# Four graph layers in one program: sources renamed to node ranks, table rows written by plain transfers, the MLP's bias added on VectorE, and the background work put in another order

## The chip, the cores and the metric

The kernel runs on one core of one Trainium2 chip. The metric is the device time of one execution in microseconds (us). Before the change three runs gave a median of 8303.18 us, the lowest 8277.47 and the highest 8350.5.

## The reference, cut to what matters

There are 6250 nodes with 128 features and 100000 edges, sorted by target. Four layers follow each other. Each takes `h = relu(layernorm(x))` and adds its result to `x`.

```python
# layer 0: graph attention, 8 heads, softmax over the edges of one target
x = layernorm(h) * gamma + beta;  x = x @ W_in + b_in
e = leaky_relu((x @ W_u + b_u)[src] + (x @ W_v)[dst])
probs = softmax of e over the edges with the same dst
out = segment_sum(x.reshape(N, 16, 8)[src] * probs[:, None, :], dst).reshape(N, 128) @ W_ff + b_ff
# layer 1: graph convolution with self loops, then batch norm over the nodes and relu
out = segment_sum((x @ W)[src] * dinv[src] * dinv[dst], dst) + b
out = relu((out - mean) * rsqrt(var + eps) * gamma + beta)
# layer 2: twice a one-head attention with self loops (W1, as1, ad1, b1), relu, (W2, as2, ad2, b2)
out = segment_sum(h[src] * softmax_by_dst(leaky_relu(alpha_s[src] + alpha_d[dst])), dst) + bias
# layer 3: a message is weighted by an edge MLP, and is summed at the SOURCE of the edge
w = silu(attr32 @ rad_W1 + rad_b1) @ rad_W2 + rad_b2 + silu(attr4 @ sph_W1 + sph_b1) @ sph_W2 + sph_b2
alpha = (q[src] * w * k[dst]).sum over 32 / sqrt(32) * edge_weight * edge_weight_n2     # 4 heads
out = segment_sum(alpha * v[dst], src)
```

## The kernel before, in words

**Ranks and columns.** The function `survey` sorts the nodes by degree. A node's place in that order is its rank. The ranks are cut into NR = 49 blocks of 128 (the index b in every loop). `node_i[:, b]` holds the node numbers of block b. Block b is given CAPS[b] edge columns (44 for the first block, 25 for the second, 9 for the last), so a block's edges fill a rectangle of 128 ranks by CAPS[b]. There are TC = 820 columns in all. `places` fills `ell`, which holds for each column the node number of the source of each of the 128 edges, or a dummy. (If the edges don't fit, another path runs. It isn't taken here.)

**Stages.** `fast0_nodes` writes the table of layer 0 (and `xv`, the node features) in the order of nodes. After it come five loops over the 49 blocks:

- g0, L1363 to L1394: layer 0. `fetch` issues one indirect gather a column (L1037) from the table into `g_x`, of which there are two buffers. VectorE makes the softmax and the sum (L1370 to L1383). Two small products follow (`times`, with `normed` between them). `by_node` (L1027) scatters the 128 new rows into table t1 with an indirect transfer from GpSimd, since the rows' places go by `node_i`.
- g1, L1407 to L1416: layer 1's gather and sum (L1411), and the mean over the nodes. After it the batch norm (L1420 to L1444), which ends in a product and a scatter into t2 for each block.
- g2 and g3, L1447 to L1475: the two attentions of layer 2. g2 scatters into t3. g3 calls `pair_rows` (L1483), which reads the MLP's result for the block's edges (`pr_e`, L1503), multiplies it by k, and writes rows of 257 numbers [w*k, lane of the source, v] into `pair_rows` in HBM: one part from SP's queue (L1509), one from ScalarE's (L1510). It also scatters q and x into `after`.
- fp, `fast_pairs` L1513: 49 blocks of nodes. 18 gathers (L1522) fetch the pairs of a block by the list `ids`, a one-hot matrix `fp_oh` (L1526) is made, transposed on TensorE (L1534), multiplied by q (L1539), and the messages are summed by matmuls (L1547).

**Background.** Three generators are advanced from within the loops by `take(generator, n)`, n steps a block:

- `weights` (`edge_weights`, 400 steps) is the edge MLP. A step does two edges for each of 125 partitions: four matmuls into `ew_h` (L1211, L1212), two SiLUs on ScalarE (L1214), six matmuls into `ew_ay` (L1218, L1219, and L1220, which adds the bias as a product of a row of ones and the bias row), and two evictions on ScalarE that scale by the edge weights (L1221). `ew_ay` and `ew_h` have one PSUM buffer each. Every second step a transpose into `ew_ay` comes first (L1201).
- `spots` (`source_places`, some 100 steps) finds each edge's place in an order by source, on VectorE.
- `ids` (`source_rows`, 820 steps) turns those places into the gather list of fp: three VectorE operations (L1289, L1292, L1293) and four matmuls (L1296) a step, with two buffers for `sr_t` and `sr_l`.

Instructions of each engine run in the order that the framework's scheduler gives them when the program is built, so `take` only proposes a place. Each DMA queue (SP, ScalarE, GpSimd) is in order too.

Of the kernel before, what the change touches and what calls it, by code (L numbers as in the profile page):

```python
# [15 lines left out]
F32 = mybir.dt.float32  # L16
# [20 lines left out]
NH, HD = 8, 16  # L37
# [805 lines left out]
def survey(k, dst):  # L843


    nc, tc = k.nc, k.tc
# [3 lines left out]
    k.odd = k.keep.tile([1, 1], I32, name="odd")  # L850
    with tc.tile_pool(name="sv", bufs=1) as p:
# [98 lines left out]
        nc.vector.tensor_copy(rl, ri)  # L950
        with tc.tile_pool(name="sv4", bufs=1) as q, tc.tile_pool(name="sv4_ps", bufs=1, space=PSUM) as ps:
# [29 lines left out]
def places(k, src):  # L981

    nc, tc = k.nc, k.tc
    line = k.dram.tile([E + RUN, 1], I32, name="src_line")
    k.ell = k.fast.tile([128, TC], I32, name="ell")
    with tc.tile_pool(name="pl", bufs=1) as p:
# [46 lines left out]
def fetch(k, p, table, b, width, name, more=0):  # L1033

    x = p.tile([128, WM + more, width], F32, name=name, bufs=2)
    for j in range(CAPS[b]):
        k.nc.gpsimd.indirect_dma_start(  # L1037
            out=x[:, j, :], out_offset=None, in_=table,
            in_offset=bass.IndirectOffsetOnAxis(ap=k.ell[:, COL[b] + j:COL[b] + j + 1], axis=0))
    return x  # L1040
# [110 lines left out]
def edge_weights(k, c, ps, src, attr32, attr4, ew1, ew2, rw1, rb1, rw2, rb2, sw1, sb1, sw2, sb2):  # L1151
# [3 lines left out]
    k.edges = k.dram.tile([E + RUN, D + 1], F32, name="edge_rows")  # L1155
    z = c.tile([RUN, D + 1], F32, name="ew_z")
# [13 lines left out]
    b2, c2 = load_row(k, c, rb2, "ew_b2", 1), load_row(k, c, sb2, "ew_c2", 1)  # L1170
    nc.vector.tensor_tensor(b2, b2, c2, op=ALU.add)
    scale = c.tile([EP, EC], F32, name="ew_scale")
    lane = c.tile([EP, EC], F32, name="ew_lane")
    with tc.tile_pool(name="ew0", bufs=1) as q:
        w = q.tile([EP, EC], F32, name="ew_w")
        nc.sync.dma_start(scale, ew1.rearrange("(p c) -> p c", p=EP))
        nc.sync.dma_start(w, ew2.rearrange("(p c) -> p c", p=EP))
        nc.vector.scalar_tensor_tensor(scale, scale, float(D3) ** -0.5, w, op0=ALU.mult, op1=ALU.mult)
        i = q.tile([EP, EC], I32, name="ew_i")
        nc.scalar.dma_start(i, src.rearrange("(p c) -> p c", p=EP))  # L1180
        j = q.tile([EP, EC], I32, name="ew_j")
        nc.vector.tensor_scalar(j, i, 127, None, op0=ALU.bitwise_and)
        nc.vector.tensor_copy(lane, j)
# [4 lines left out]
    for c0 in range(0, EC, KC):  # L1188
# [5 lines left out]
        for t in range(0, KC, 2):  # L1194
# [9 lines left out]
            if t % KO == 0:  # L1204
                out = c.tile([EP, KO, D + 1], F32, name="ew_out", bufs=2)
                nc.vector.tensor_copy(out[:, :, D], lane[:, c0 + t:c0 + t + KO])
# [8 lines left out]
            for n in range(2):  # L1215
# [3 lines left out]
                nc.tensor.matmul(y, lhsT=g[:, 1, e], rhs=s2, start=False, stop=False)  # L1219
                nc.tensor.matmul(y, lhsT=k.ones[0:1, :EP], rhs=b2, start=False, stop=True)  # L1220
                nc.scalar.activation(out[:, t % KO + n, 0:D], y, AF.Identity, scale=scale[:, c0 + t + n:c0 + t + n + 1])  # L1221
            if (t + 2) % KO == 0:
                at = (c0 + t + 2 - KO) * (D + 1)
                by_engines(nc.sync.dma_start, to[:, at:at + KO * (D + 1)], out.rearrange("p c f -> p (c f)"))
            yield


def source_places(k, c, q, acc):
# [4 lines left out]
    k.lane3 = c.tile([128, TC], F32, name="sp_lane")  # L1233
    b = q.tile([128, TC], I32, name="sp_b")
    nc.vector.tensor_scalar(b, k.ell, 7, None, op0=ALU.logical_shift_right)
# [32 lines left out]
    w, x = q.tile([128, TC], I32, name="sp_w"), q.tile([128, TC], I32, name="sp_x")  # L1268
    nc.vector.tensor_copy(w, pos)
    nc.vector.tensor_scalar(x, w, 7, None, op0=ALU.logical_shift_right)  # L1270
    nc.vector.tensor_copy(k.tile3, x)
    nc.vector.tensor_scalar(x, w, 127, None, op0=ALU.bitwise_and)
    nc.vector.tensor_copy(k.lane3, x)
# [3 lines left out]
def source_rows(k, c, acc):  # L1277
# [9 lines left out]
    for cc in range(TC):  # L1287
        t = c.tile([128, TT], F16, name="sr_t", bufs=2)
        nc.vector.tensor_scalar(t, it, k.tile3[:, cc:cc + 1], None, op0=ALU.is_equal)  # L1289
        l = c.tile([128, 2, 128], F16, name="sr_l", bufs=2)  # L1290
# [21 lines left out]
def fast_layers(k, x, src, edges, l0, l1, l2a, l2b, l3, after):  # L1312
# [3 lines left out]
    with ExitStack() as ctx:  # L1316
# [9 lines left out]
        xp = c.tile([128, NR, D + NH], F32, name="xp")  # L1326
        own = c.tile([128, NR, D + 2], F32, name="own")
# [11 lines left out]
        for n, a in enumerate(l3[8:11]):  # L1339
            for h in range(H3):  # L1340
                s = slice(h * D3, (h + 1) * D3)
                nc.sync.dma_start(w4[s, n, s], a[h])
        k.pairs = k.dram.tile([(TC + 1) * 128, 2 * D + 1], F32, name="pair_rows")
        none = c.tile([128, 2 * D + 1], F32, name="pair_none")
        nc.gpsimd.memset(none, 0.0)
        nc.gpsimd.memset(none[:, D:D + 1], -1.0)
# [9 lines left out]
                               mlp.enter_context(tc.tile_pool(name="mlp_ps", bufs=1, space=PSUM)), src, *edges, *l3[0:8])  # L1356
# [3 lines left out]
        with tc.tile_pool(name="g0s", bufs=1) as ps0, \  # L1360
                tc.tile_pool(name="g0", bufs=2) as p, tc.tile_pool(name="g0_ps", bufs=2, space=PSUM) as ps:
            spots = source_places(k, later, ps0, places3)
            for b in range(NR):  # L1363
# [4 lines left out]
                rows = fetch(k, p, t0, b, D + NH, "g0_x")  # L1368
# [23 lines left out]
                by_node(k, t1, own[:, b, 0:D], b, "t1")  # L1392
                take(spots, 3)
                take(weights, 3)  # L1394
            take(spots, 3 * NR)

        ids = source_rows(k, later, places3)

        with tc.tile_pool(name="g1", bufs=2) as p:
# [5 lines left out]
            with tc.tile_pool(name="g1_st", bufs=1, space=PSUM) as ps1:  # L1405
                mean = ps1.tile([128, D], F32, name="g1_mean")
                for b in range(NR):  # L1407
                    n = CAPS[b]
                    rows = fetch(k, p, t1, b, D, "g1_x")
# [227 lines left out]
```

## Time and profile before

| What | Value |
|---|---|
| median of 3 runs | 8303.18 us |
| profiled execution: its own time, its span | 8362.09 us, 8360.3 us |
| PE, weight loads, DVE, ACT, POOL busy | 50%, 34%, 40%, 20%, 56% |
| mean granted TensorE clock | 0.627 |
| HBM | 420.83 MB read, 186.20 MB written, 73 GB/s |
| gathers by L1037 | 3280, mean 1.0 to 1.1 us on POOL |
| gathers by L1522 | 882, mean 1061 ns |

POOL is GpSimd, PE is TensorE, DVE is VectorE, ACT is ScalarE, SP is the sync engine whose queue issues plain transfers. Idle time of an engine is put down to what ended it. "issue" means that the profile shows nothing that the engine waited for. No engine is busy through the whole span, and the stages differ, so the table alone says little: times are to be read by stage.

### The profile page before, as it was taken

To read this page: it belongs to the slowest core of one execution; us is meant where nothing else is said; L and a number is where in the kernel's file an instruction comes from. 1 tells how busy PE (TensorE), PEld (TensorE's weight loads), DVE (VectorE), ACT (ScalarE), POOL (GpSimd) and SP (SyncE) were. 2 spreads that over 40 slices of the span, in tenths; PEclk is the share of its full clock that TensorE was granted. 3 is DMA by queue.
4 is the path that set the end of the run, shared out by engine and by line. 5 is a ranking of instruction groups with operands and counts; after the bars stand their busy time and mean duration, and the time that the engine had idled before them with its cause. 6 is when DMAs were issued, how large, how long until landed. Compare 5 with 4: busy or idle time off the path is not lost. (4 is left out here: it accounts for less than half of the span.)

```text
span 8360.3 us, 55810 instructions
## 1 busy us (share of the span) xinstructions
PE 4209.2 (50%) x17979; PEld 2860.6 (34%) x17979; DVE 3377.0 (40%) x6506; ACT 1638.4 (20%) x3582; POOL 4708.7 (56%) x4551
## 2 busy tenths in 40 slices
PE   2314555666466456766556789942100002554555
PEld 2213344443233334544333455620000002444444
DVE  9535455443222222434333454334433343434344
ACT  0202233332111111342222233301111111000000
POOL 0166777664545555345666761046777775667665
PEclk9555555667655555775555669965555555777777
DMA  0222222222111111122222221048888884333333
GB/s 4 67 47 51 56 58 56 54 55 41 50 43 50 44 48 50 42 47 50 48 55 51 59 52 39 27 70 162 163 156 164 153 162 104 93 92 93 93 93 81
DMA packets 440385, 611.13 MB, mean 73 GB/s; under 512 B 88306, under 2 KB 332388, under 8 KB 436487
## 3 DMA queue, kind: packets, MB, share of 16 engines
q0 software_dynamic: 164688, 409.60, 20.9%
q1 hardware_dynamic: 169128, 143.04, 8.1%
q10 hardware_dynamic: 106254, 54.71, 4.0%
q8 instruction: 147, 2.41, 0.1%
q14 instruction: 168, 1.37, 0.1%
HBM read 420.83 MB, written 186.20 MB: 73 GB/s over the span
## 5 line engine op out<-in xcount | busy, mean ns | idle before, releaser
L1037 POOL DMA_INDIRECT g_x<-l_t,ell x1640 | 1661.6, 1013 | 1066.4 <-issue 485.7
L1296 PE MATMUL sr_acc<-sr_t,sr_l 128*128 128x441 f16 x3280 | 1111.2, 455 | 567.2 <-DVE sr_l L1292 287.0
L1037 POOL DMA_INDIRECT g_x<-l2b_t,ell x820 | 898.0, 1095 | 765.7 <-DVE sr_l L1293 373.7
L1289 DVE TENSOR_SCALAR sr_t<-sr_it,sp_tile 128x882 f16<-128x882 f16 x820 | 378.1, 461 | 2204.9 <-PE sr_acc L1296 1032.4
L1522 POOL DMA_INDIRECT fp_rows<-pair_rows,ids x882 | 935.5, 1061 | 447.7 <-issue 260.6
L1037 POOL DMA_INDIRECT g_x<-l2a_t,ell x820 | 835.5, 1019 | 352.1 <-issue 262.6
L1218 PE MATMUL ew_ay<-ew_r,ew_g 128*125 128x128 f32 x1600 | 478.9, 394 | 954.9 <-issue 460.7
L1218 PEld LDWEIGHTS ew_ay<-ew_r,ew_g 128*125 128x125 f32 x1600 | 366.1, 266 | 1158.9 <-issue 520.4
L1221 ACT ACTIVATE ew_out<-ew_ay,ew_scale 125x128 f32<-125x128 f32 x800 | 293.8, 367 | 2237.0 <-remote 987.5
L1296 PEld LDWEIGHTS <-sr_l 128*128 128x128 f16 x3280 | 337.8, 117 | 928.6 <-DVE sr_l L1292 333.2
L1211 PE MATMUL ew_h<-ew_aT,ew_r 128*128 128x125 f32 x1600 | 516.9, 416 | 100.8 <-ACT ew_aT L1203 50.6
L1212 PE MATMUL ew_h<-ew_dT,ew_s 40*128 40x125 f32 x1600 | 522.0, 418 | 18.4 <-issue 11.0
L1220 PE MATMUL ew_ay<-ew_b,ones 1*125 1x128 f32 x1600 | 522.3, 418 | 0.0
L1061 PE MATMUL tm_ty<-ident,pr_h 128*128 128x128 f32 x49 | 22.4, 459 | 859.4 <-ACT pr_h L1054 545.0
L1219 PE MATMUL ew_ay<-ew_s,ew_g 128*125 128x128 f32 x1600 | 425.6, 360 | 5.3 <-ACT ew_g L1214 4.3
L1211 PEld LDWEIGHTS ew_h<-ew_aT,ew_r 128*128 128x128 f32 x1600 | 329.7, 256 | 274.6 <-issue 136.6
L1464 DVE TENSOR_REDUCE g_a<-g_x 128x128 f32<-128x2176 f32 (+17 forms) x98 | 409.2, 4176 | 0.0
L1454 DVE TENSOR_SCALAR g_e<-g_x,own 128x17 f32<-128x17 f32 (+17 forms) x98 | 24.6, 251 | 942.1 <-DMA g_x<-l2b_t,ell 715.0
L1539 PE MATMUL fp_qe<-fp_qx,fp_ot 128*128 128x128 f32 x1764 | 314.0, 341 | 177.6 <-ACT fp_ot L1536 110.9
L1212 PEld LDWEIGHTS ew_h<-ew_dT,ew_s 40*128 40x128 f32 x1600 | 326.7, 253 | 169.4 <-issue 112.5
L1219 PEld LDWEIGHTS ew_ay<-ew_s,ew_g 128*125 128x125 f32 x1600 | 373.7, 273 | 22.5 <-ACT ew_g L1214 4.6
L1536 ACT COPY fp_ot<-fp_tr 128x512 f32<-128x512 f32 (+1 forms) x245 | 126.0, 545 | 1262.4 <-remote 444.8
(263 smaller groups left out, 6936.2 us busy)
## 6 DMA issues: line engine op xcount, KB each, us to landing
edge_rows<-ew_out SPq DMA_DIRECT2D x80, 564.4 KB
g_x<-l_t,ell POOLq DMA_INDIRECT x1640
fp_rows<-pair_rows,ids POOLq DMA_INDIRECT x882
g_x<-l2a_t,ell POOLq DMA_INDIRECT x820
g_x<-l2b_t,ell POOLq DMA_INDIRECT x820
ew_a<-in_edge_attr_dram SPq DMA_DIRECT2D x40, 280.0 KB
fp_qx<-after SPq DMA_DIRECT2D x49, 128.0 KB
pair_rows<-pr_e SPq DMA_DIRECT2D x5, 1225.5 KB
```

Source lines behind the costliest of these rows:

```text
L1037: k.nc.gpsimd.indirect_dma_start(out=x[:, j, :], out_offset=None, in_=table, in_offset=bass.IndirectOffsetOnAxis(ap=k.ell[:, COL[b] + j:CO ...
L1211: nc.tensor.matmul(h[:, 0, e], lhsT=r1[:, (t + n) % 4, :], rhs=aT, start=True, stop=True)
L1212: nc.tensor.matmul(h[:, 1, e], lhsT=s1[:, (t + n) % KO, :], rhs=dT, start=True, stop=True)
L1218: nc.tensor.matmul(y, lhsT=g[:, 0, e], rhs=r2, start=True, stop=False)
L1219: nc.tensor.matmul(y, lhsT=g[:, 1, e], rhs=s2, start=False, stop=False)
L1220: nc.tensor.matmul(y, lhsT=k.ones[0:1, :EP], rhs=b2, start=False, stop=True)
L1221: nc.scalar.activation(out[:, t % KO + n, 0:D], y, AF.Identity, scale=scale[:, c0 + t + n:c0 + t + n + 1])
L1289: nc.vector.tensor_scalar(t, it, k.tile3[:, cc:cc + 1], None, op0=ALU.is_equal)
L1296: nc.tensor.matmul(acc[:, n, h, 0:HT], lhsT=l[:, n, :], rhs=t[:, h * HT:(h + 1) * HT], start=(cc == 0), stop=(cc == TC - 1))
L1464: nc.vector.tensor_reduce(a, v.rearrange("p w d -> p d w"), axis=AX.X, op=ALU.add)
L1522: nc.gpsimd.indirect_dma_start(out=rows[:, t, :], out_offset=None, in_=k.pairs, in_offset=bass.IndirectOffsetOnAxis(ap=k.ids[:, h * TB + t ...
L1539: nc.tensor.matmul(qe[:, t, :], lhsT=ot[:, t, :], rhs=qx[:, 0:D], start=True, stop=True)
```

## The change

**Ranks instead of nodes.** A new generator, `source_ranks` (82 steps and a start), runs during g0. It turns the source numbers of all 820 columns into ranks, ten columns a step: a broadcast row of the sources' low seven bits comes from HBM through SP's queue, one VectorE operation makes one-hots of it, ten matmuls look up `rank_b`, and VectorE picks the block and adds (L1264 to L1274 of the new file). From g1 on the gathers go by `ranks`, so table rows lie in rank order and block b's rows are 128 rows in a line. The scatters into t1, t2 and t3 become plain transfers on SP's queue (`by_rank`). `places` and the tables of layer 0 stay in node order.

**q and x stay on chip.** `after` is not written in this path. `own` keeps q and `xp` keeps x, in a pool that lives to the end. fp reads them there. Since blocks are now of ranks, the output is scattered by `node_i` from GpSimd, once a block, where it was a plain transfer from SP.

**Edge MLP.** The two bias matmuls of a step and the two scaling evictions on ScalarE go away. One VectorE addition of 125x256 from PSUM adds the bias. The edge weight rides along as one more number of the edge row (130 instead of 129, pair rows 258 instead of 257), and fp multiplies `al` by it (245 small VectorE operations).

**Order.** `ranks` 2 and `weights` 4 a block in g0; `weights` 5 and `spots` 3 in g1, where whatever is left of both is then taken; `mlp.close()` stands before g2; `ids` 9 a block in g2 and g3. `sr_t` and `sr_l` get four buffers. g1's gather tile is 25 columns wide instead of 44, so its first block comes in two parts.

```diff
-def fetch(k, p, table, b, width, name, more=0):
+def fetch(k, p, table, ids, b, width, name, more=0, part=None):
...
-            in_offset=bass.IndirectOffsetOnAxis(ap=k.ell[:, COL[b] + j:COL[b] + j + 1], axis=0))
+            in_offset=bass.IndirectOffsetOnAxis(ap=ids[:, COL[b] + j:COL[b] + j + 1], axis=0))
...
-                out = c.tile([EP, KO, D + 1], F32, name="ew_out", bufs=2)
-                nc.vector.tensor_copy(out[:, :, D], lane[:, c0 + t:c0 + t + KO])
+                out = c.tile([EP, KO, D + 2], F32, name="ew_out", bufs=2)
+                nc.vector.tensor_copy(out[:, :, D:D + 2], scale[:, c0 + t:c0 + t + KO, None].to_broadcast([EP, KO, 2]))
...
-                nc.tensor.matmul(y, lhsT=g[:, 1, e], rhs=s2, start=False, stop=False)
-                nc.tensor.matmul(y, lhsT=k.ones[0:1, :EP], rhs=b2, start=False, stop=True)
-                nc.scalar.activation(out[:, t % KO + n, 0:D], y, AF.Identity, scale=scale[:, c0 + t + n:c0 + t + n + 1])
+                nc.tensor.matmul(y, lhsT=g[:, 1, e], rhs=s2, start=False, stop=True)
+            nc.vector.tensor_tensor(out[:, t % KO:t % KO + 2, 0:D], ay[:EP, 256:512].rearrange("p (n d) -> p n d", n=2),
+                                    b2[:, None, :].to_broadcast([EP, 2, D]), op=ALU.add)
...
+def source_ranks(k, c, acc):
...
+    for n, c0 in enumerate(range(0, TC, KC)):
+        m = min(KC, TC - c0)
+        row = c.tile([128, KC * 128], BF16, name="rk_row", bufs=2)
+        nc.sync.dma_start(row[:, 0:m * 128], lanes[c0:c0 + m, :].rearrange("(o c) e -> o (c e)", o=1).to_broadcast([128, m * 128]))
+        oh = c.tile([128, KC * 128], BF16, name="rk_oh", bufs=2)
+        nc.vector.tensor_scalar(oh[:, 0:m * 128], row[:, 0:m * 128], own, None, op0=ALU.is_equal)
+        y = acc[:, n % 2, :, 0:490].rearrange("p s (c v b) -> p s c v b", c=5, v=2)
+        for j in range(m):
+            nc.tensor.matmul(y[:, j // 5, j % 5], lhsT=oh[:, j * 128:(j + 1) * 128], rhs=k.rank_b, start=True, stop=True)
+        ob = c.tile([128, KC, NR], F32, name="rk_ob")
+        nc.vector.tensor_tensor(ob[:, :m], k.iota_l[:, None, :NR].to_broadcast([128, m, NR]),
+                                hi[:, c0:c0 + m, None].to_broadcast([128, m, NR]), op=ALU.is_equal)
+        pr = c.tile([128, KC, 2, NR], F32, name="rk_pr")
+        for j0 in range(0, m, 5):
+            w = min(5, m - j0)
+            nc.vector.tensor_tensor(pr[:, j0:j0 + w], y[:, j0 // 5, 0:w], ob[:, j0:j0 + w, None, :].to_broadcast([128, w, 2, NR]), op=ALU.mult)
+        r = c.tile([128, KC, 2], F32, name="rk_r")
+        nc.vector.tensor_reduce(r[:, :m], pr[:, :m], axis=AX.X, op=ALU.add)
+        f = c.tile([128, KC], F32, name="rk_f")
+        nc.vector.scalar_tensor_tensor(f[:, :m], r[:, :m, 1], 128.0, r[:, :m, 0], op0=ALU.mult, op1=ALU.add)
+        nc.vector.tensor_tensor(k.ranks[:, c0:c0 + m], f[:, :m], none[:, c0:c0 + m], op=ALU.add)
+        yield
...
-        t = c.tile([128, TT], F16, name="sr_t", bufs=2)
+        t = c.tile([128, TT], F16, name="sr_t", bufs=4)
...
-        l = c.tile([128, 2, 128], F16, name="sr_l", bufs=2)
+        l = c.tile([128, 2, 128], F16, name="sr_l", bufs=4)
...
+def by_rank(k, table, rows, b):
+
+    k.nc.sync.dma_start(table[b * 128:(b + 1) * 128, :], rows)
...
-                by_node(k, t1, own[:, b, 0:D], b, "t1")
-                take(spots, 3)
-                take(weights, 3)
-            take(spots, 3 * NR)
-
-        ids = source_rows(k, later, places3)
+                by_rank(k, t1[:, :], own[:, b, 0:D], b)
+                take(ranks, 2)
+                take(weights, 4)
+            take(ranks, TC)
...
-                    take(weights, 3)
-                    take(ids, 6)
+                    take(weights, 5)
+                    take(spots, 3)
+                take(weights, EC)
+                take(spots, 3 * NR)
...
-                        by_node(k, t2, own[:, b, 0:D + 1], b, "t2")
+                        by_rank(k, t2, own[:, b, 0:D + 1], b)
+        mlp.close()
+        ids = source_rows(k, ctx.enter_context(tc.tile_pool(name="sr", bufs=1)), places3)
...
-                        by_node(k, t3, own[:, b, 0:D + 1], b, "t3")
-                        take(weights, 3)
+                        by_rank(k, t3, own[:, b, 0:D + 1], b)
                     else:
-                        pair_rows(k, p, ps, xp[:, b, 0:D], a, w4, b, after)
-                    take(ids, 6)
-                if name == "g2":
-                    take(weights, EC)
-            if name == "g2":
-                mlp.close()
+                        nc.vector.tensor_tensor(xp[:, b, 0:D], xp[:, b, 0:D], a, op=ALU.add)
+                        pair_rows(k, p, ps, xp[:, b, 0:D], own[:, b, 0:D], w4, b)
+                    take(ids, 9)
...
-            qx = p.tile([128, 2 * D], F32, name="fp_qx")
-            nc.sync.dma_start(qx, after[h * 128:(h + 1) * 128, :])
...
+                nc.vector.tensor_tensor(al[:, ts, :], al[:, ts, :], rows[:, ts, D:D + 1].to_broadcast([128, nt, H3]), op=ALU.mult)
...
-            nc.sync.dma_start(out[h * 128:h * 128 + n, :], y[0:n, :])
+            st = nc.gpsimd.indirect_dma_start(
+                out=out, out_offset=bass.IndirectOffsetOnAxis(ap=k.node_i[0:n, h:h + 1], axis=0), in_=y[0:n, :], in_offset=None)
```

## The prediction

> **What bounds the kernel now.** I read the page's 40 slices first, because no engine is busy through the whole span.
>
> ```profile
> PE   2314555666466456766556789942100002554555
> POOL 0166777664545555345666761046777775667665
> PEclk9555555667655555775555669965555555777777
> DMA  0222222222111111122222221048888884333333
> ```
>
> GpSimd (POOL) is busy in six or seven tenths of most slices, TensorE (PE) in five or six at about half its clock. From slice 27 the DMA engines are at eight tenths. So the limits change by stage, and I cut the span at the stages' first and last gathers. The columns are window, length, busy time and count of PE, weight loads, VectorE, ScalarE and GpSimd, then PE clock, DMA share and GB/s. In order the rows are g0, g1, batch norm, g2, the gap before g3, g3, fp; the first 457 us lie before them.
>
> ```profile
> 457.00:1956.00 1499.00, 839.29 (x2799) 567.15 (x2800) 735.87 (x1387) 466.37 (x892) 974.65 (x911) 0.55 0.23 54
> 1956.00:3457.00 1501.00, 842.77 (x3001) 547.28 (x3001) 367.02 (x739) 181.31 (x486) 781.50 (x821) 0.59 0.19 47
> 3457.00:3661.00 204.00, 198.16 (x1051) 139.75 (x1052) 119.15 (x498) 141.93 (x325) 48.78 (x49) 0.90 0.12 38
> 3661.00:5101.00 1440.00, 933.59 (x3188) 580.77 (x3186) 559.93 (x1125) 353.05 (x782) 892.52 (x869) 0.59 0.23 52
> 5101.00:5475.00 374.00, 373.53 (x1971) 234.26 (x1970) 127.46 (x467) 115.80 (x312) 0.67 (x1) 1.00 0.10 30
> 5475.00:6946.00 1471.00, 208.07 (x493) 70.45 (x491) 597.87 (x947) 208.81 (x425) 1005.52 (x919) 0.53 0.80 150
> 6946.00:8360.00 1414.00, 695.59 (x4410) 630.52 (x4410) 550.10 (x834) 127.26 (x246) 936.31 (x883) 0.72 0.36 91
> ```
>
> In the gap GpSimd does nothing for 374 us while PE is busy throughout: what is left of the edge MLP stands ahead of g3. An undisturbed gather takes 0.95 us plus 0.30 us of issue, so 820 of them need 1025 us. g1 takes 1501. The waits inside g1 (total, times, longest) say why:
>
> ```profile
> DVE sr_t L1289 <- PE sr_acc L1296: 509.9, 95, 40.1
> POOL g_x L1037 <- DVE acc L1411: 227.1, 18, 39.6
> POOL g_x L1037 <- DVE sr_l L1292: 133.8, 5, 28.8
> POOL g_x L1037 <- DVE sr_l L1293: 83.9, 5, 30.8
> ```
>
> VectorE (DVE) is busy only 367 us, but in its order the `ids` steps stand waiting for PE. The sum that frees a gather buffer stands behind them, and GpSimd loses 445 us. PE is the hidden bound of g0 to g2, through waits on VectorE.
>
> PE's pace hangs on its clock. The timeline gives one fp32 matmul of the MLP (two instructions): its pitch is 0.715 us in g1 and 0.41 us in the gap.
>
> ```profile
> 2314.43 0.79 PE L1212 MATMUL ew_h<-ew_dT,ew_s 40*128 40x125 f32 x2
> 2315.14 0.79 PE L1211 MATMUL ew_h<-ew_aT,ew_r 128*128 128x125 f32 x2
> 5202.01 0.48 PE L1212 MATMUL ew_h<-ew_dT,ew_s 40*128 40x125 f32 x2
> 5202.42 0.49 PE L1211 MATMUL ew_h<-ew_aT,ew_r 128*128 128x125 f32 x2
> ```
>
> The groups of lines price what goes away:
>
> ```profile
> L1220 PE MATMUL ew_ay<-ew_b,ones 1*125 1x128 f32 x1600 | 522.3, 418 | 0.0
> L1221 ACT ACTIVATE ew_out<-ew_ay,ew_scale 125x128 f32<-125x128 f32 x800 | 293.8, 367 | 2237.0 <-remote 987.5 <-PE ew_ay L1220 891.7 <-issue 247.9
> L1027 POOL DMA_INDIRECT l2b_t<-own,node_i x49 | 57.7, 1178 | 197.4 <-DVE own L1470 152.8 <-DVE g_s L1460 22.7 <-issue 12.1
> ```
>
> **The MLP step.** Two of ten matmuls go, 522 us of PE in all, and two ScalarE evictions (294 us), which lay beside PE. In their place comes a VectorE addition of 125x256 from PSUM. No row shows that size. It lies between 0.35 us (L1391, 128 numbers from PSUM) and 0.63 us (L1541, 512 numbers); I take 0.42, so 400 cost 168 us of VectorE. The dearer part is its wait: `ew_ay` has one buffer, so each addition stands in VectorE's queue until PE has ended the step. A cold step is eight matmuls by 0.715, or 5.7 us, plus two SiLUs by 0.47 and half a transpose with its copy (about 0.8): 7.5 us. At full clock it is 3.3 + 1.1 + 0.8 = 5.2 us.
>
> **g0: 1500 us (1250 to 1700).** In the order of the built program 164 MLP steps and the 82 `ranks` steps stand before g1's first sum. MLP: 164 by 7.5 is 1230 us. A ranks step has ten bf16 matmuls, which no row prices: between 0.1 us (half a cold fp32 instruction, 0.36, were it all width) and 0.36 each; at 0.2, 820 make 164 us. The block's own small products add some 100. PE's sum is 1494, and GpSimd's is lower: 820 gathers by 1.31 and 49 of `xp` by 1.4, 1143. A ranks step costs VectorE about 4.0 us (a one-hot 0.6, its block one-hot 0.6, two products of 490 numbers from PSUM by 0.63, a reduction 1.2, small ones 0.3), 328 in all. Added to about 490 of g0's own and 70 of MLP additions that fills 890 of 1500. The scatters' 50 us and their 140 us of waiting on GpSimd go, but PE decides. The low end has a clock that is full half the time, the high end steps of 8.7 us.
>
> **g1: 1200 us (1040 to 1400).** The ids steps leave, and with them the 445 us of lost gathers: 1501 - 445 = 1056. In come 113 MLP steps (848 us cold, fits) and some 60 `spots` steps on VectorE (1 to 3 us each). An addition that waits up to 7.5 us now stands ahead of a block's sum. Two buffers of 25 columns cover 31 us, but in the last blocks, of 9 columns, only 11. I add back a third of the waits, 145 us. The ends: none returns, or nearly all.
>
> **Batch norm: 240 (204 to 290).** 33 MLP steps by 7.5 are 248, by 5.2 are 172; VectorE and ScalarE keep their work.
>
> **A tail ahead of g2: 590 (470 to 675).** 164 + 113 + 33 = 310 of 400 steps. In the built order the last 90 follow the batch norm, before g2's first VectorE work, with no ids matmuls between them (their tiles reuse the MLP's memory). GpSimd has only block 0's 44 gathers to do beside it. 90 steps by 5.2 are 470, by 7.5 are 675; I take a little above the middle. The old gap ran 66 MLP steps and 152 ids steps in its 374 us, so the gap moves ahead of g2 and loses its filler.
>
> The full clock there isn't certain. The granted clock was 1.00 in the gap, where PE was busy 99.9%, and 0.50 at 2310 to 2345 us, among waits. The Trainium skill, "TensorE: Matmul & The Clock Gate", Part 1, says that full rate comes only after a sustained busy window and is lost when PE idles. A pure MLP tail waits for SiLUs in every step, so by this rule it could fall back to the cold 675; by the gap's row alone it would be 470.
>
> **g2: 1210 (1100 to 1350).** The scatters go: 58 us, and the 153 + 23 us that GpSimd stood in them waiting for rows. So does a 61 us wait for `ew_aT`: 1440 - 295 = 1145. ids doubles to nine a block, 9 us of VectorE in a block of about 24, with four buffers in place of two. Gathers of g2 took 1019 ns in the mean beside 221 ids steps, 57 us more in all than at 0.95; I add 65, those 57 for as many steps again and 8 for sums that come late. PE carries 441 steps of at most 1.8 us, under 800. If no such wait comes back, 1100; if 200 us do, 1350.
>
> **The gap: 374 to 0.** Nothing of the MLP is left.
>
> **g3: 1440 (1400 to 1600).** The DMA engines stay at 0.80. The `after` scatters (55 us of GpSimd, 37 of waiting) leave. About 300 more ids steps put 310 us on VectorE, 600 to 910 of 1440. GpSimd's queue hides part of the gain behind DMA, so I take 30 off; the high end is late sums.
>
> **fp: 1475 (1430 to 1560).** 49 output scatters join 882 gathers in GpSimd's queue, at 1.05 + 0.30 = 1.35 us: 66 us. Each waits for its block's `fp_y`, with the next gathers behind it. The built order puts three blocks of gathers between, more than the delay that the wait view shows (`PE fp_acc`, 136 us in 19 waits, longest 10.6). 245 multiplications of `al` by 0.16 are 40 us of VectorE, idle 860 us there. q's loads go.
>
> That VectorE slows gathers is seen beside `fp_oh` (2.54 us): one gather took 2.48 us where 0.95 is usual. The Trainium skill, "SBUF — State Buffer", Who interferes with whom, says that VectorE and GpSimd share a port pair which some VectorE operations lock whole, shutting out the other engine. That speaks against moving ids under the gathers of g2 and g3: were each of some 510 more steps there (1.03 us of VectorE) a lock that GpSimd runs into, the rule's worst case would be 525 us; by the row of g2 (57 us for 221 steps) they cost about 130, half of it in g3, where DMA covers it.
>
> **Sum.** 470 + 1500 + 1200 + 240 + 590 + 1210 + 0 + 1440 + 1475 = 8125, where 470 is the opening with ten or so microseconds of setup more. The profiled execution took 8362.09 for a span of 8360.3; the median 8303.18 is 0.993 of it. 8125 by 0.993 is 8068, say 8070: 2.8% faster.
>
> **Rivals.**
>
> - *VectorE in line behind PE* (slower, 0.29). 277 additions wait in g0 and g1, as 95 `sr_t` waits did at 5.4 us each in the row above. If ranks and additions queue so that a step takes 8.7 us, g0 is 1700. If the 445 us in g1 return but for 100, it is 1400. With a cold tail of 675: 470 + 1700 + 1400 + 240 + 675 + 1210 + 1440 + 1475 = 8610, by 0.993 is 8550. It decides from about 8.2 us a step. For it: the chain of one buffer, and g1's old waits. Against: two matmuls fewer.
> - *Gathers alone set g0 to g2* (0.22, counted as faster). A full clock: 470 + 1400 + 1100 + 220 + 470 + 1150 + 1430 + 1430 = 7670, by 0.993 is 7620. For it: 1025 us of gathers. Against: PE clock 0.55 to 0.59 there.
> - *The stall only moves* (within 1%, 0.14). A cold tail of 675, g0 at 1560, g1 at 1250, g2 at 1270: 8380, by 0.993 is 8320. For it: 590 to 675 us of tail against 374 us of gap.
>
> My forecast's case has 0.35, its own range 7850 to 8220. Faster by over 1% is 0.35 + 0.22 = 0.57. One per cent is about what three runs (8277 to 8350) can tell apart. Range 7620 to 8600.
>
> **What would show it.** g1 near 1200 with `DVE acc` waits small; an empty GpSimd stretch of 470 to 675 us between batch norm and g2; no gap before g3; g0 unchanged with PE the releaser of VectorE. I am wrong if GpSimd waits in g1 stay over 400 us, if the tail runs under g2's gathers, or if fp grows by over 100.

## The result, and the profile after

The changed kernel takes 8391.68 us (median of 10 runs), the kernel before 8301.02 beside it: ratio 1.010, interval 1.007 to 1.013. The forecast was 8070, 2.8% faster; it is 1% slower. The profiled execution took 8350.31 us, its span 8348.4. The page's slices of the changed kernel:

```profile
PE   2314556666544444788824444543344524454545
POOL 0166454445467665200057666667777766666665
PEclk9555555555555555565556666665666757777777
DMA  0232222222222111110022111147777763333332
```

In the 18th to 20th slice GpSimd stands still, as it nearly did in the 25th and 26th before. But where PE then ran at full clock, it now runs at a little over half. The stages, by the same windows and columns as before (g0, g1, batch norm, tail, g2, g3, fp):

```profile
455.00:2153.00 1698.00, 945.80 (x3793) 724.16 (x3793) 800.39 (x1558) 451.12 (x854) 850.65 (x862) 0.52 0.26 70
2153.00:3441.00 1288.00, 626.37 (x2058) 470.70 (x2058) 461.19 (x547) 118.62 (x317) 826.84 (x820) 0.51 0.21 57
3441.00:3645.00 204.00, 181.85 (x807) 142.29 (x807) 90.36 (x342) 150.74 (x305) 0.00 (x0) 0.69 0.16 45
3645.00:4207.00 562.00, 455.06 (x1493) 340.39 (x1492) 39.87 (x107) 90.31 (x242) 0.00 (x0) 0.51 0.09 26
4207.00:5494.00 1287.00, 558.62 (x1894) 224.46 (x1895) 711.87 (x1757) 59.70 (x199) 865.46 (x822) 0.64 0.21 45
5494.00:6851.00 1357.00, 525.29 (x1682) 201.65 (x1679) 801.80 (x1836) 229.50 (x482) 990.57 (x869) 0.65 0.74 160
6851.00:8348.00 1497.00, 735.17 (x4410) 679.43 (x4410) 576.07 (x1078) 129.17 (x245) 988.53 (x931) 0.71 0.31 81
```

| us | before | forecast | changed | changed, run e9 |
|---|---|---|---|---|
| opening | 457 | 470 | 455 | 457 |
| g0 | 1499 | 1500 | 1698 | 1357 |
| g1 | 1501 | 1200 | 1288 | 1084 |
| batch norm and tail | 204 | 830 | 766 | 764 |
| g2 (the gap before g3 for itself) | 1440 + 374 | 1210 | 1287 | 1150 |
| g3 | 1471 | 1440 | 1357 | 1409 |
| fp | 1414 | 1475 | 1497 | 1289 |
| span | 8360 | 8125 | 8348 | 7510 |

(The last column is explained with run e9.) The timeline shows why GpSimd is empty for all of batch norm and tail, the last lines of the tail and the first gather of g2:

```profile
4202.44 0.75 SPq L1154 DMA_DIRECT2D edge_rows<-ew_out  x2
4206.40 0.30 ACT L1516 COPY g_x<-own 128x129 f32<-128x129 f32 x1 [6.21 <-DMA edge_rows<-ew_out]
4207.08 0.94 POOL L1043 DMA_INDIRECT g_x<-l2a_t,ranks  x1 [773.71 <-ACT g_x L1516]
```

The MLP's last result is written out, only then does ScalarE write into `g_x`, and only then do the gathers start. The MLP's memory has been handed on to g2, so its last transfer is a barrier before all of g2. The next two lines are GpSimd's waits for VectorE's sums in g0 (51.6 us before) and in g1:

```profile
POOL g_x L1043 <- DVE g_a L1439: 472.3, 30, 31.0
POOL g_x L1043 <- DVE g_s L1471: 209.3, 19, 26.3
```

### The profile page after: what moved, and what is told of

It is laid out like the page before. It is cut to its first block, busy times and chain, and to the rows that moved or that the text cites. A ratio compares the mean times of both kernels' runs of the same rounds, so it can differ in the third digit from the quotient of the medians.

```text
span 8348.4 us, 54643 instructions
## 1 busy us (share of the span) xinstructions
PE 4148.0 (50%) x17206; PEld 2875.2 (34%) x17206; DVE 3801.1 (46%) x7733; ACT 1273.0 (15%) x2758; POOL 4590.8 (55%) x4405
## 5 line engine op out<-in xcount | busy, mean ns | idle before, releaser
L1349 PE MATMUL sr_acc<-sr_t,sr_l 128*128 128x441 f16 x3280 | 1002.5, 465 | 1284.8 <-DVE sr_l L1345 591.3
L1043 POOL DMA_INDIRECT g_x<-l2a_t,ranks x820 | 864.4, 1054 | 1178.5 <-ACT g_x L1516 916.3
L1043 POOL DMA_INDIRECT g_x<-l_t,ell x820 | 812.8, 991 | 783.8 <-DVE g_a L1439 472.3
L1043 POOL DMA_INDIRECT g_x<-l2b_t,ranks x820 | 931.6, 1136 | 312.6 <-issue 239.4
L1043 POOL DMA_INDIRECT g_x<-l_t,ranks x820 | 826.8, 1008 | 455.7 <-issue 235.3
L1220 DVE TENSOR_TENSOR ew_out<-ew_ay,ew_b 125x256 f32<-125x256 f32 x400 | 169.3, 423 | 1828.5 <-PE ew_ay L1219 1027.4
L1595 PE MATMUL fp_qe<-own,fp_ot 128*128 128x128 f32 x1764 | 339.6, 349 | 467.7 <-DVE fp_pr L1597 361.0
L1595 PEld LDWEIGHTS fp_qe<-own,fp_ot 128*128 128x128 f32 x1764 | 302.5, 255 | 501.3 <-DVE fp_pr L1597 361.8
L1214 ACT ACTIVATE ew_g<-ew_h,ew_b 128x250 f32<-128x250 f32 x400 | 187.7, 469 | 1620.5 <-PE ew_h L1212 757.2
L1604 PE MATMUL fp_acc<-fp_rows,fp_oh 128*128 128x128 f32 x1764 | 325.8, 331 | 99.7 <-issue 93.7
```

Source lines behind the costliest of these rows:

```text
L1043: k.nc.gpsimd.indirect_dma_start(out=x[:, j - first, :], out_offset=None, in_=table, in_offset=bass.IndirectOffsetOnAxis(ap=ids[:, COL[b] ...
L1214: nc.scalar.activation(g[:, n, :], h[:, n, :], AF.Silu, bias=bias)
L1349: nc.tensor.matmul(acc[:, n, h, 0:HT], lhsT=l[:, n, :], rhs=t[:, h * HT:(h + 1) * HT], start=(cc == 0), stop=(cc == TC - 1))
L1595: nc.tensor.matmul(qe[:, t, :], lhsT=ot[:, t, :], rhs=k.own[:, h, 0:D], start=True, stop=True)
L1604: nc.tensor.matmul(acc, lhsT=oh[:, t, :], rhs=rows[:, t, D + 2:2 * D + 2], start=(t == 0), stop=(t == TB - 1))
```

## The experiments

Ratios are against the kernel before, run on the same chip beside the kernel. Stage times are those of each profiled execution.

### The addition, and the ranks: two suspects for g0

**e2_add_alone**: the kernel before, with

```diff
-                nc.tensor.matmul(y, lhsT=g[:, 1, e], rhs=s2, start=False, stop=False)
-                nc.tensor.matmul(y, lhsT=k.ones[0:1, :EP], rhs=b2, start=False, stop=True)
-                nc.scalar.activation(out[:, t % KO + n, 0:D], y, AF.Identity, scale=...)
+                nc.tensor.matmul(y, lhsT=g[:, 1, e], rhs=s2, start=False, stop=True)
+            nc.vector.tensor_tensor(out[:, t % KO:t % KO + 2, 0:D], ay[...], b2[...], op=ALU.add)
```

> The kernel before with one part of the change alone: an MLP step's two bias matmuls and two ScalarE evictions give way to one VectorE addition from PSUM. It leaves out the scaling of the MLP's result by the edge weight. Theory A (VectorE stands in line behind PE): PE loses 522 us of work, but 400 additions now wait for PE in VectorE's order, ahead of the sums that free gather buffers, so g0 doesn't get shorter than 1499 by more than 50 us and GpSimd's wait for the g0 sum, 52 us before, goes over 100; in all between -150 and +100 us against 8303. Rival R (the ranks steps alone lengthened g0): the addition costs nothing and the matmuls' time is a gain: g0 falls by 80 us or more, in all -200 to -400 us.

Ratio 0.956 (0.951 to 0.961). g0 and g1 together took 2887 us where they took 2997 before. The gap before g3 is all but gone:

```profile
5089.00:5112.00 23.00, 17.68 (x63) 7.53 (x64) 17.16 (x56) 1.64 (x6) 4.17 (x5) 0.68 0.31 109
```

With the 522 us of bias matmuls gone from PE, the MLP ends within g2. Theory A falls here: the addition alone is a gain of 4.4%, and GpSimd's wait for the g0 sum fell from 51.6 to 31.6 us. Its wait for the g1 sum did rise, from 227.1 to 387.4 us, but g0 and g1 got shorter all the same.

**e3_act_evict**: the changed kernel, with

```diff
-            nc.vector.tensor_tensor(out[:, t % KO:t % KO + 2, 0:D], ay[...], b2[...], op=ALU.add)
+            nc.scalar.copy(out[:, t % KO:t % KO + 2, 0:D], ay[...])
             if (t + 2) % KO == 0:
+                nc.vector.tensor_tensor(out[:, :, 0:D], out[:, :, 0:D], b2[...], op=ALU.add)
```

> The changed kernel, but ScalarE copies an MLP step's result out of PSUM, and VectorE adds the bias once for ten edges (80 additions of 125x1280 numbers in SBUF in place of 400 of 125x256 from PSUM). VectorE then waits for the MLP in one step of five. Theory A: g0 falls from 1697 us to 1500-1600, GpSimd's wait for the g0 sum from 472 to under 250 us, g1 from 1282 to about 1200; in all 150 to 300 us under the changed kernel's 8392. Rival R (ranks): g0 stays over 1640 and the total within 80 us of 8392. The tail ahead of g2 stays near 560 us by both.

Ratio 1.003 (0.999 to 1.006); g0 1718 us with 164 MLP steps, so no shorter. The waits of its g0 show that VectorE's wait took another name: the product of a ranks step, with a releaser that the profile calls "remote" (more on it below). GpSimd waited less for g_a, but g0's end didn't come sooner:

```profile
DVE rk_pr L1269 <- remote: 241.8, 27, 51.8
POOL g_x L1043 <- DVE g_a L1439: 278.8, 22, 25.5
```

**e4_no_ranks**: the changed kernel, with

```diff
-            ranks = source_ranks(k, q, places3)
-                take(ranks, 2)
-            take(ranks, TC)
+            nc.vector.tensor_copy(k.ranks, k.ell)
```

> The changed kernel without the ranks steps: the list of ranks is a copy of the list of nodes, so as many rows of the same size are gathered, but others. It leaves out the 82 steps that turn sources into ranks (328 us of VectorE work, 90 us of PE). Rival R: the ranks steps hold up the g0 sums, so g0 falls from 1697 us to 1500 or less and GpSimd's wait for the g0 sum from 472 to under 150 us; in all about -200 us. Theory A: the additions' waits stay, g0 falls by 100 us at most, to 1600-1690. If both parts share the cost, g0 lies near 1600 here and in the kernel with ScalarE's eviction alike.

Ratio 1.018 (1.014 to 1.022): slower, with less work. g0 fell to 1425 us, but it held only 111 MLP steps where it had 160: `take` only proposes, and the scheduler had put them elsewhere. Batch norm and tail held 171 in place of 123 and took 1068 us in place of 766. So 273 us left g0 and 302 came back in batch norm and tail: g0 can't be judged without counting its steps.

### The tail

**e5_mlp_g2**: the changed kernel, with

```diff
-                take(weights, EC)
                 take(spots, 3 * NR)
...
-        mlp.close()
-        ids = source_rows(k, ctx.enter_context(tc.tile_pool(name="sr", bufs=1)), places3)
+        ids = source_rows(k, ctx.enter_context(tc.tile_pool(name="sr", bufs=1, side="right")), places3)
...
                         by_rank(k, t3, own[:, b, 0:D + 1], b)
+                        take(weights, 2)
...
+            if name == "g2":
+                take(weights, EC); mlp.close()
```

> The changed kernel with the MLP kept open through g2: what is left of its 400 steps after the batch norm (90) is taken two a block in g2 and no longer ahead of it; the pool of the ids steps lies at the other end of the memory. Theory T (the tail is a barrier: g2's gathers wait for its last write, and it lies alone): the 562 us between batch norm and g2 fall to under 20; PE was idle 728 of g2's 1287 us, so g2 grows by 100 to 250; in all -300 to -450 us, to 7950-8100. Rival (PE's work is only moved, and VectorE waits for it in g2 as in g0): g2 grows by 400 to 560 and the total stays within 150 us of 8392.

Ratio 0.965 (0.960 to 0.970). The tail is gone (batch norm 214 us), and g2 took

```profile
3716.00:5165.00 1449.00, 802.59 (x3311) 452.40 (x3310) 732.34 (x1801) 201.84 (x476) 836.86 (x820) 0.70 0.21 50
```

and 18 us up to g3: 1467 for 1287, so 180 us for 89 MLP steps, 2.0 each. In the tail a step cost 562 / 90 = 6.2 us. Theory T holds; the place of the last 90 steps is worth 4.5% (1.010 to 0.965).

**t2_two_bufs**: the changed kernel, with

```diff
-            ay = ps.tile([128, 512], F32, name="ew_ay")
+            late = c0 + t >= 620 and t % 4 == 2
+            ay = k.spare[:, 1, 0, :] if late else ps.tile([128, 512], F32, name="ew_ay")
```

and the same for `h`, where `k.spare` is `sr_acc`.

> The changed kernel with a second place in PSUM for the two tiles of an MLP step (in the four banks that ids will use later), taken by every second step of the last 90, so that PE can begin a step while ScalarE and VectorE end the one before. Nothing else. Theory K (the tail is slow because PE idles 19% of it, in every step, and so runs at half its clock): PE stays busy, the granted clock rises from 0.51 to over 0.8, and the tail falls from 562 us to 330-420; in all -130 to -230 us against the changed kernel. Rival L (only the waits of the chain count): the waits go, the clock stays near 0.5 and eight cold matmuls and the transposes of 5.7 to 6.2 us a step keep the tail at 500-550.

Ratio 0.986 (0.981 to 0.990). The tail fell from 562 to 351 us (87 steps for 90), the granted clock in it rose from 0.51 to 0.74:

```profile
3655.00:4006.00 351.00, 320.51 (x1444) 247.68 (x1444) 38.74 (x104) 85.57 (x235) 0.00 (x0) 0.74 0.14 41
```

PE does nearly the same matmuls (1444 for 1493) in 321 us that took 455: 134 of the 211 us are faster matmuls, the rest is idle time of PE that went. Theory K holds, though its clock of over 0.8 wasn't reached: 4.0 us a step is less than eight cold matmuls (5.7). Busy 81% of the tail PE was at half clock; busy 91%, at three quarters.

### What fills g0

**f1_no_mlp_g0** (no `take(weights, 4)` in g0, four a block in g2; the MLP open through g2), **f2_bare_g0** (that, without ranks steps), **f3_floor** (that, with the MLP set up after g0) and **f4_two_g0** (e5 with `take(weights, 2)` in g0 and three in g2):

> The kernel with the MLP kept open through g2, and no MLP step asked for in g0 (ranks stay there); g1 asks for five a block and g2 for four. Theory C (an MLP step costs what it costs: PE's cold chain of 5 to 6 us is not hidden in g0, wherever the step's eviction runs): g0 falls from about 1700 us to 1200-1300, near GpSimd's 1143; each step that moves to g2, where the clock is higher and ids matmuls fill the gaps, costs 2 to 4 us there; in all 7750 to 8000. Rival R (the ranks steps hold up g0): g0 stays at 1500 or more, the total above 8050.

> As the run without MLP steps in g0, and without the ranks steps too: the list of ranks is a copy of the list of nodes, so as many rows of the same size are gathered, but others. It leaves out the turning of sources into ranks. Both theories: g0 at its floor, set by 820 gathers and 49 loads on GpSimd, 1143 to 1250 us. What it is above the run with ranks gives the price of the ranks steps alone: under 60 us by theory C, 250 us or more by rival R. If g0 stays over 1350 here, the block's own chain sets it and both are wrong.

> As the run without MLP and ranks steps in g0, but the MLP is set up only after g0, so none of its steps can come forward into it. It leaves out the turning of sources into ranks. From four runs (160 MLP and 82 ranks steps: 1697 us; 9 and 82: 1390; 111 and 0: 1425; 70 and 0: 1350) a straight line gives 1.8 us for an MLP step, 1.9 for a ranks step, and 1222 us with none. If the costs add, g0 is 1190 to 1250 here. If g0 lies over 1320, its own gathers and sums hold it and the two backgrounds share one cost; under 1170 the first MLP steps cost more than the later ones.

> The kernel with the MLP kept open through g2, with two MLP steps asked for in a block of g0 in place of four, five in g1, three in g2. By the line g0 is 1222 + 82 x 1.9 + n x 1.8, for n of 80 to 105 steps 1522 to 1567 us. If the two backgrounds only hinder each other when both are dense, g0 is under 1470; if either alone fills it, over 1620. In all within 1% of the run with four (0.965 of the kernel before), as steps cost about 2 us in g2 as well.

| run | MLP steps in g0 | ranks steps | g0, us |
|---|---|---|---|
| f3 | 0 | 0 | 1214 |
| f2 | 70 | 0 | 1350 |
| f1 | 9 | 82 | 1390 |
| e4 | 111 | 0 | 1425 |
| f4 | 96 | 82 | 1487 |
| changed | 160 | 82 | 1698 |

The floor came where the line put it, 1214 for 1222. f4 came some 60 us under the line, f1 90 above theory C's range. So neither theory: each background alone costs about 1.9 us a step above the floor (f2 136 us for 70, e4 211 for 111, f1 176 for 91), the first 87 MLP steps beside the ranks cost 97 us, 1.1 each (f1 to f4), and the last 64 cost 211 us, 3.3 each. The rows (f3, f1, f4), with PE busy 237 us of 1390 in f1 and 645 of 1487 in f4, show that PE is not full there. So steps wait. Whether they wait for each other, as they get denser, or for PE standing still, these runs don't separate; run e9 below bears on it.

```profile
472.00:1686.00 1214.00, 119.82 (x294) 65.89 (x294) 458.18 (x767) 169.00 (x315) 901.04 (x854) 0.50 0.24 52
455.00:1845.00 1390.00, 236.99 (x1265) 165.71 (x1266) 733.50 (x1378) 226.26 (x383) 888.99 (x862) 0.50 0.29 67
454.00:1941.00 1487.00, 645.18 (x2733) 490.12 (x2733) 771.88 (x1483) 386.83 (x679) 871.42 (x863) 0.52 0.30 72
```

Whole times: f1 0.982 (0.976 to 0.988), where some 74 of the MLP's steps fell into a gap of 332 us before g3; f2, one run, 7948 us; f3, one run, 8067, with the same gap. f4, with 154 MLP steps in g2 at clock 0.75 and no gap, 0.943 (0.931 to 0.954).

### The other stages

**e6_plain_out**: in fp, `nc.sync.dma_start(out[h * 128:h * 128 + n, :], y[0:n, :])` for the scatter.

> The changed kernel with the output written by plain transfers from SP's queue, once a block. It leaves out putting the rows back in the order of the nodes. Theory F (the 49 scatters on GpSimd and the gathers behind them are what fp lost): the last stage falls from 1497 us to 1414-1440. Rival (the multiplication by the edge weight, in VectorE's chain between PE's products, lost it): it stays over 1475.

fp fell to 1425 us, by 72; ratio 0.9995 (0.997 to 1.002). Theory F holds: what fp lost is the 49 scatters in GpSimd's queue; with the multiplications by the edge weight still in, fp is within 11 us of the 1414 before.

```profile
6965.00:8390.00 1425.00, 725.84 (x4410) 674.51 (x4410) 576.98 (x1078) 129.35 (x245) 942.87 (x882) 0.72 0.33 85
```

**e7_before_258**: the kernel before, with `D + 2` and `2 * D + 2` for the widths of both tables.

> The kernel before with rows of 130 and 258 numbers in the MLP's and the pairs' tables in place of 129 and 257 (the lane is stored twice), nothing else. Theory W (g3 got 114 us shorter in the changed kernel because rows of 1032 bytes are written faster than rows of 1028): g3 falls from 1471 us to 1340-1400, and ScalarE's queue of transfers takes a fifth less time for the same bytes. Rival (the leaving scatters into the table of q and x made it shorter): g3 stays between 1450 and 1490.

Between the two: g3 took 1426 us (from the first gather of g3 to that of fp; 1487 before by the same cut), ScalarE's queue 3.8% of the engines' time where it had 4.0%. Ratio 0.991 (0.988 to 0.994). But e2 and b2 (below), with 228 and 226 ids steps in g3 and rows of 257 and 258 numbers, took 1470 and 1458 us there. So the whole time shows an effect of the size of the rows, and how much of g3's gain it makes stays open: the changed kernel's g3 alone took 1357 us in one profile and 1409 in another (e9), and the scatters of q and x were not tried alone.

### Better versions

**b2_mlp_part**: the kernel before with the whole MLP part (e2 and e7, the edge weight in the row, `al` multiplied by it). **b3_mlp_part_act**: that, with e3's eviction. **b1_comb**: e5 with e3's eviction. **f5_best**: f4 with e3's eviction.

> The kernel before with the MLP part of the change alone, whole this time: one VectorE addition a step, the edge weight as one more number of a row (130 and 258 numbers), and the multiplication of al by it in the last stage. The order of the background, the ranks and the scatters stay as before. If the parts add up: 0.956 for the addition, about -0.009 for the row size, and 0 to +0.005 for 245 small multiplications on a VectorE that is 38% busy there: 0.945 to 0.955 of the kernel before, and so the fastest. If the multiplications delay the last stage by their length and its waits, 0.96 or more.

> The same MLP part on the kernel before, but with ScalarE copying a step's result out of PSUM and VectorE adding the bias once for ten edges. In this kernel VectorE has spots, ids and the sums in g0 and g1, and GpSimd waited 387 us for the g1 sum with the addition alone. Theory A, in the one place left to it: that wait falls by 100 us or more and the total by 50 to 120 us against the addition from PSUM. Rival: ids steps hold VectorE up, not additions: within 30 us of it.

> The kernel with the MLP kept open through g2, and with ScalarE's eviction and one addition of VectorE for ten edges. The eviction alone took 0.7% off the changed kernel, with g0 no shorter. If the additions cost little anywhere, as g0 said, the total is within 60 us of the run with the MLP kept open (0.965 of the kernel before). If VectorE's wait for PE matters in g2, where ids and additions meet, g2 falls from 1449 us to under 1400 and the total to 0.955.

> The kernel with the MLP open through g2 and two steps a block in g0, and ScalarE's eviction with one addition for ten edges beside it. ScalarE's eviction took 0.4% where it was tried with the MLP open, so 0.937 to 0.943 of the kernel before. If g0 and g2, now less dense, leave VectorE idle enough, it brings nothing: 0.943 to 0.947.

b2 0.946 (0.942 to 0.950): the MLP part alone is worth 5.4%, as the parts add up. b3 0.942 (0.937 to 0.946): GpSimd's wait for the g1 sum fell from 361.5 to 189.9 us, as theory A asks, but the two intervals overlap. b1 0.961 (0.956 to 0.965) overlaps with e5 as well. f5 0.935 (0.933 to 0.937), 6859 us beside 7335 for the kernel before. It beats both kernels; whether e3's eviction has a share in that stays open, as f4 was measured under other conditions, which the next runs explain.

### Standstills of PE

**e9_after_again** (the changed kernel, unaltered) and **b4_part_again** (b3, unaltered):

> The changed kernel once more, unaltered. In the run before this one the kernel before took 7335 us and not some 8350, and the waits on PE that the profile can put down to nothing on this core were gone from the profile of its partner. If they are gone here too: g0 near 1350, the tail still 560 us (it holds no such wait), and, as the tail weighs more in a shorter run, 1.02 to 1.04 of the kernel before. If they are back: 1.01 as on record.

> The MLP part of the change alone on the kernel before, with ScalarE's eviction, once more, on the same chip as the changed kernel: 0.937 to 0.946 of the kernel before if the waits on PE are back. Without them the gap that it saves (374 us of 7335) weighs more, and what it saves of PE less: 0.93 to 0.95.

During these two and f5, every kernel was 10 to 13% faster, the one before too (7362 us here, 7335 beside f5), so only ratios are compared across. The changed kernel: 7518 us, 1.021 (1.020 to 1.023). b4: 0.948 (0.946 to 0.950). The difference is in waits that the profile calls "remote", for it finds no cause on this core. One in g1 of the changed kernel on record:

```profile
2406.52 0.79 PE L1212 MATMUL ew_h<-ew_dT,ew_s 40*128 40x125 f32 x2
2423.85 0.42 DVE L1220 TENSOR_TENSOR ew_out<-ew_ay,ew_b 125x256 f32<-125x256 f32 x1 [38.50 <-remote]
2427.42 0.47 ACT L1214 ACTIVATE ew_g<-ew_h,ew_b 128x250 f32<-128x250 f32 x1 [24.45 <-remote]
```

PE's records end at 2407, but VectorE starts on one step's result at 2424 and ScalarE on the next one's at 2427: PE, or the passing on of its results, had stood still for some 17 us; the profile doesn't tell which. In e9 no such wait is listed, and g0 took 1357 us with the same 160 and 82 steps, 341 less:

```profile
457.00:1814.00 1357.00, 937.06 (x3794) 718.91 (x3794) 797.57 (x1558) 451.47 (x855) 885.88 (x864) 0.53 0.36 87
POOL g_x L1043 <- DVE g_a L1439: 134.4, 21, 11.7
```

PE's busy time and clock are nearly the same in both (937 and 946 us, 0.53 and 0.52). What differs is GpSimd's wait for VectorE's sums: 134.4 us for 472.3 in g0, and none listed in g1 where it was 209.3. These 338 and 209 us are the 341 and 204 us by which the two stages got shorter. By this account PE's late results held up VectorE's order, and through it the gathers; no run switched them on or off by intent. Denser steps still cost something: f5's g0, with two steps a block asked for and e3's eviction, took 1246 us.

The tail took what it had taken (764 us with batch norm, for 766), as it holds no such wait. So the loss on record doesn't hang on the standstills; without them the tail weighs more. Beside b4, the kernel before with the MLP part, e9's span is 532 us longer (7510 to 6978), and batch norm and tail make 525 of them. They took 764 us where b4's batch norm took 239:

```profile
2849.00:3088.00 239.00, 229.58 (x1302) 162.24 (x1301) 151.07 (x599) 171.51 (x366) 54.54 (x50) 0.92 0.14 42
```

What makes PE stand still was not found.

## Why the prediction was wrong

- **Its sign.** The sum of 8125 missed the span by 223 us: g0 +198, g1 +88, g2 with the rest of the gap +77, fp +22, less opening -15, batch norm and tail -64, g3 -83. The other 100 of the 322 us between 8070 and 8392 come from the factor 0.993. The kernel before had been profiled in one of its longest executions, the changed one in its shortest (its factor is 1.005). A single profile's ratio to the median is no property of the next kernel. The rival *The stall only moves* came nearest with 8320, but its g0 (1560) was too short and its tail (675) too long.
- **g0 is the step that failed.** "PE decides", with 164 steps by 7.5 us (a sum of 1494 us), was the wrong kind of sum: g0 took 1698 us and PE was busy 946 of them. The runs show another bill: a floor of 1214 us (f3), and on top of it, as nearly all of the other 484, the 472.3 us that GpSimd waits for VectorE's sums (17.1 in f3). "The scatters' 140 us of waiting go, but PE decides" let a gain fall and priced no new wait. The waits called remote stood in the trace before and got no term. These two are from its g0 and its g1:

```profile
ACT ew_out L1221 <- remote: 216.6, 23, 28.3
DVE sr_t L1289 <- remote: 487.0, 37, 51.0
```

The prediction shows only the 509.9 us that `sr_t` waited for PE. Without waits called remote GpSimd's wait in g0 is 134.4 us and the stage 341 us shorter, 1357. The rival *VectorE in line behind PE* named the place (additions in line behind PE) and the stage (1700), but the additions alone aren't the cause: with four of five off VectorE g0 was 1718. The ranks steps were priced high on PE: 164 us, where 90.4 were measured.

- **g1 and g2** lost the waits that were named, and more came back than was added: 209 us in g1 for the sums, where 145 were allowed. Without the standstills (e9) g1 lists no such wait, and the two stages took 1084 and 1150 us, less than the forecast 1200 and 1210.
- **The tail** was forecast at 590 and took 562, at clock 0.51. That the two are close is luck: the clock was the cold one, for which the forecast had 675, and the cold price of 7.5 us a step was too high; 6.2 was measured. (Its 1.1 us for two SiLUs at full clock should have been 0.94.) The rule of the Trainium skill ("TensorE: Matmul & The Clock Gate", Part 1) pointed the right way against the row of the gap, and t2 goes with it: clock 0.74 once most idle spaces were filled. The stretch from 2310 to 2345 us doesn't. The prediction puts it "among waits", but PE was busy 34.64 of its 35 us and the clock was 0.50:

```profile
2310.00:2345.00 35.00, 34.64 (x108) 22.99 (x109) 10.21 (x22) 5.85 (x16) 10.33 (x11) 0.50 0.14 39
```

Block 0's gathers were to run beside the tail: they didn't, the memory held them back.

- **The gap** went, as forecast. Its 374 us turned into 562: the same kind of steps, without the ids matmuls between them and at half the clock. By e5 the place of these steps is worth 4.5%, most of what the MLP part gains by itself (5.4%).
- **g3** was put too high: that wider rows could be a gain was not seen. That VectorE slows the gathers was put at 130 us by the row of g2, and came to half: gathers took 1054 ns in g2 and 1136 in g3, 35 and 41 more than before, 62 us in all, far from the worst case of 525.
- **fp** was right in its mechanism: 72 us of scatters for 66 forecast.

## What to carry to other kernels

Count the steps of a background in every stage before a stage is judged, since a scheduler moves them when their neighbours change. Work that must end before a buffer's memory is handed on becomes a barrier: put it where other work can share PE, and not by itself in a row (PE's clock was 0.70 in e5's g2 and 0.51 in the tail). A step that is cheap among others (2.0 us in e5's g2) can cost three times that alone (6.2).

## What the runs showed of the hardware

- PE's granted clock went with small idle spaces in the tail: busy 81% it was 0.51, busy 91% it was 0.74, for nearly the same matmuls. Being busy is not all: in g1 of the kernel before it was 0.50 for 35 us with PE busy 99%, and in the gap 1.00 with PE busy 99.9%.
- PE's results can reach the engines behind it well after PE's own records end (some 17 us in the example). The engines then show waits called remote, up to 50.4 us long in the changed kernel. In the profiles of three runs these were missing, and their kernels and the kernel before were 10 to 13% faster. In the changed kernel they were listed in the stages with gathers, and not in batch norm or the tail.
- Rows of 1032 and 520 bytes in place of 1028 and 516 made the kernel before 0.9% faster (0.6 to 1.2%).
